# Key sums merged over two steps, scatters without a chain, and a replanned layer: one change to a two-layer recurrent-style kernel

## The chip, the cores and the metric

The kernel runs on one core of a Trainium2 chip. The metric is the device time of one execution in microseconds (us), the median of the runs shown. Profiles are of one execution each, with the time that it took.

## What is computed

Input `x` is [2, 2048, 256] in fp32, everything is fp32. Two layers, each `x = x + s * silu(f)`, on a layer norm of `x` without weights:

```
# layer 0
xn = layernorm(x)
s  = linear_attention(xn)                      # elu+1 features with rotary positions, 16 heads of 16, then @ W_out
h  = layernorm(xn)*ln1_g + ln1_b
y  = xn + softmax_attention(h) @ Wproj         # causal, rotary positions, 16 heads of 16, 2048 keys
h2 = layernorm(y)*ln2_g + ln2_b                # 4096 tokens
gates = softmax(h2 @ Wgate)                    # 8 experts, the best 2 of each token
pos = place of the token in its expert, in the order of the tokens   # room for 1024 a piece
moe = sum of both experts: gelu(h2 @ W1[e] + b1[e]) @ W2[e] + b2[e], times gate, none where pos >= 1024
x  = x + s * silu(y + moe)
# layer 1
xn = layernorm(x)
s  = softmax_attention(xn; q, k, v of 32 per head, 16 heads, causal) @ Wo
x  = x + s * silu(xn @ int4(kernel) + bias + xn @ a @ b)
```

## The kernel before, in words

There are three stages, in this order: layer 0 with both its attentions and the routing, the eight experts, layer 1.

**Attention in steps.** `run_attention` works for both layers. A group is one batch and four heads, eight groups in a layer. For a group and a chunk `c` of 256 queries, *pass A* (L534) forms scores of a tile of 128 queries against up to 512 keys, and DVE takes their maximum (L545, or L541 on the diagonal). `subtract` turns the maxima and folds them in: in layer 0 into `qt` (L782), in layer 1 by six small Pool instructions (L1433 to L1435), a turn (L1439), a copy (L1446) and a bf16 matmul on each score tile (L1453). *Pass B* (L560) forms the scores again with the keys on the partitions, two tiles of 128 keys (a pair `p`) at once, hides the future (L504), and ACT takes exp into `pt` (L572). Then `sum_keys` forms the sums over the keys: the weights of one `p` against `vt` (layer 0 L792, layer 1 L1466). In layer 0 `vt` carries a column of ones, so the sum of the weights comes with it. In layer 1 the heads fill all 32 columns; Pool adds the two key tiles (L1472, with a copy L1474 on the diagonal) into `ps`, and TensorE sums `ps` over the partitions (L1478, the total). DVE adds each result into `un` (L800; L1484). `finish` normalises, and in layer 0 calls `residual` (L841, L848) and, for every second chunk of the last group, `route`.

Scores use TensorE as four tiles of 32 rows, one head each. Sums use it as four tiles of 32 columns. All other work ("guests": projections, turns, linear attention, gates) uses the full array.

A step `u` of the loop has one pass A tile set and one pass B pair, four score tiles each, and the sums of an earlier step: two steps later in layer 0, three in layer 1 (`SUM_LAG`).

**The planner.** Every operation is a `Step` with an engine, an estimated cost, and what it reads and writes. `Plan.run` orders them by a beam search over a model of the engines, buffers and tiling modes, with handicaps by strand ("prep", "end", "moe", ...), and the program is then issued in that order by hand, with no other scheduler. Sums and scores are the main strand ("S") on TensorE. A guest may enter only in front of a main step that is marked open; before the change the first score of every step is open. The 8 PSUM banks `s` are shared by all. Parts of the linear attention are released by step number (`others`): batch 0 from step 4 on, batch 1 from step 150, one every 8 steps.

**Routing.** `route` takes four tiles of 128 tokens: statistics (L475, `roots` on Pool, L461), scaled tokens into `x2` (one slot), a turn and the gate matmul (L911), the choice of two experts and the places (small DVE instructions, a count on TensorE, L943), then eight indirect DMAs from Pool's queue (L972) that scatter rows to `slots_in` in DRAM. Each writes `slots_in`, and so waits for the one before to land. The experts load `xe` from `slots_in` (L1261), turn it (L1266), and multiply (L1272, L1278).

**Layer 1's start.** `mix` (L1332 to L1350) fetches each token's two expert rows with four indirect DMAs per two tiles, weighs and gates them; eight such parts for batch 0 come first, eight for batch 1 run beside the attention of batch 0, all partly on Pool.

Of the kernel before, what the change touches and what calls it, by code (L numbers as in the profile page):

```python
# [110 lines left out]
class Plan:  # L111
# [25 lines left out]
    BEAM, TRIALS, SPREAD = 4, 8, 0.4  # L137
# [180 lines left out]
def kernel(ctx: ExitStack, tc: tile.TileContext, i: dict, out: bass.AP):  # L318
# [60 lines left out]
    v8 = w0.tile([8, P], F32, name="v8")  # L379
    for n, name in enumerate(("ln1_g", "ln1_b", "ln2_g", "ln2_b")):  # L380
        nc.sync.dma_start(v8[2 * n : 2 * n + 2], i[f"L0_ffn_{name}"].rearrange("(k p) -> k p", p=P))
    b64 = w0.tile([E * 8, P], F32, name="b64")
# [17 lines left out]
    with tc.tile_pool(name="prelude", bufs=1) as pool:  # L400
        for n, c in enumerate((C_ID, C_AFTER)):
            m = bank().rearrange("p (q n) -> p q n", q=4)
            for q in range(4):
                rep = pool.tile([P, 4, 32], F32, name=f"rep{n}{q}")
                nc.vector.tensor_copy(
                    rep, ident[:, None, 32 * q : 32 * q + 32].to_broadcast([P, 4, 32])
                )
                nc.tensor.matmul(
                    m[:, q], rep.rearrange("p j d -> p (j d)"), cst[:, c : c + P], start=True, stop=True
                )  # L410
            if n == 0:
                nc.vector.tensor_copy(ident_h, m)
            else:
                nc.vector.tensor_copy(mask_h, m[:, :, None].to_broadcast([P, 4, 2, P]))
        tp = bank("t")
        nc.tensor.transpose(tp[:, :8], v8, ident[:8, :8])
        nc.vector.tensor_copy(cols, tp[:, :8])
        tp = bank("t")
        nc.tensor.transpose(tp[:, : E * 8], b64, ident[: E * 8, : E * 8])
        nc.vector.tensor_copy(b1c, tp[:, : E * 8])  # L420
# [33 lines left out]
    def norms(w, S):  # L454
# [4 lines left out]
        def root(dst, src, tmp):  # L459

            nc.gpsimd.tensor_tensor(dst, src, minus_half, ALU.pow)  # L461
            nc.gpsimd.tensor_tensor(tmp, dst, dst, ALU.mult)
            nc.gpsimd.tensor_tensor(tmp, tmp, src, ALU.mult)
            nc.gpsimd.tensor_scalar(tmp, tmp, -0.5, 1.5, ALU.mult, ALU.add)
            nc.gpsimd.tensor_tensor(dst, dst, tmp, ALU.mult)

        st, ag = w.tile([P, 4, 6], F32, name="ln_st"), w.tile([P, 4, 2], F32, name="ln_ag")
        va, tmp = w.tile([P, 4], F32, name="ln_v"), w.tile([P, 4], F32, name="ln_t")

        def stats4(strand, n0, name, r, m, r1=None):  # L470
            r, m = r[:, n0 : n0 + 4], m[:, n0 : n0 + 4]

            def moments():
                for n in range(4):
                    nc.vector.bn_stats(st[:, n], xr[:, n0 + n])  # L475
                for n in range(4):
                    nc.vector.bn_aggr(ag[:, n], st[:, n])

            def roots():
# [4 lines left out]
                if r1 is not None:  # L484
# [3 lines left out]
                    root(r1[:, n0 : n0 + 4], va, tmp)  # L488

            S(strand, "DVE", 2.2, moments, r=[("xr", n0 + n) for n in range(4)], w=["ln"])  # L490
            S(strand, "POOL", 2.4, roots, r=["ln"], w=["ln", (name, n0)])

        return stats4

    LAG = 1
    SUM_LAG = 3
# [16 lines left out]
    def run_attention(plan, make, prepare, subtract, sum_keys, finish, last_sum, before=None, others=()):  # L513
# [65 lines left out]
        sums, parts_left = {}, []  # L579
        for u in range(at + last_sum + 1):  # L580
# [29 lines left out]
            if first:  # L610
                first.open = True
            if a and t == 2 * c + 1 and k == t // 4:
                subtract(g, c, mx, parts)
            if b:
                for n, call in sum_keys(gb, cb, p, pt):
                    sums.setdefault(u + n, []).append(call)
                if p == cb:
                    sums[u + last_sum].append(lambda gb=gb, cb=cb: finish(gb, cb))
# [8 lines left out]
            while parts_left and u >= due:  # L627
                parts_left.pop(0)()
                due += every

# [4 lines left out]
    ps_first.close()  # L635
    with ExitStack() as sc:
# [13 lines left out]
        for vt in vts:  # L650
# [25 lines left out]
                x2=slots(wk, "x2", 1, [P, 4, D]), xl=slots(wk, "xl", 1, [P, 2, D]),  # L676
            ),
            dict(prep=-0.5, sub=-0.5, end=-0.2, moe=-0.1),
        )
        S = plan.step  # L680
        stats4 = norms(w, S)

        def normalise0(n0):
# [9 lines left out]
            stats4("prep", n0, "r", ln_r, ln_m, ln_r1)  # L693
# [90 lines left out]
        def sum_keys(G, c, p, pt):  # L784
            if p == 0:
                G.sums[c] = Buf("un")
            un, av = G.sums[c], Buf("s")

            def add():
                for n, (kj, q0, at) in enumerate(halves_of(c, p)):  # L790
# [828 lines left out]
```

## Time and profile before

| | us |
|---|---|
| median of 3 runs (lowest, highest) | 3627.52 (3627.36, 3629.56) |
| profiled execution | 3629.38 |
| its span, first to last instruction | 3627.6 |
| TensorE clock granted, mean | 0.961 of full |
| layer 0: last matmul of the key sums (L792) begins to end | 1439.8 to about 1441 |
| first expert matmul (L1272) | 1545.06 |

In lines of the page, `out<-in` are the program's names; "x" is a count; then follow the busy time in us, the mean of one in ns, and after the bar the idle time of the engine just before these instructions with what ended most of it. PE is TensorE's matmuls, PEld its weight loads, POOL is GpSimd. One fp32 matmul gives two matmul records. In a timeline or a chain, the first number is the start in us, the second the length.

### The profile page before, as it was taken

How to read it: one execution, taken by the hardware profiler on the slowest of the kernel's cores; microseconds unless marked ns; L12 is line 12 of the kernel's file. 1: busy time of each engine (PE TensorE's matmuls, PEld its weight loads, DVE VectorE, ACT ScalarE, POOL GpSimd, SP SyncE). 2: the span in 40 equal slices, each digit the busy share in tenths (PEclk: the TensorE clock that was granted, in tenths of full speed). 3: DMA queues.
4: the chain of work that ended last, by engine and by line, in shares of the span. 5: the costliest groups of instructions: out<-in, count | busy, mean ns of one | idle time of the engine just before them, and what ended most of it. 6: DMA issues, size and time to landing. Idle time of an engine off the chain costs nothing.

```text
span 3627.6 us, 83893 instructions
## 1 busy us (share of the span) xinstructions
PE 3423.8 (94%) x34834; PEld 2340.2 (65%) x34834; DVE 2311.2 (64%) x5937; ACT 1659.7 (46%) x3278; POOL 1395.6 (38%) x2134
## 2 busy tenths in 40 slices
PE   6999999999999999199999599999999999999999
PEld 4667777776677776166666356666666666666666
DVE  4777787878787877211111267777777657777776
ACT  2565555555555555011111155445445444444444
POOL 4453223333322212200000455666554345555555
PEclk7999999999999999599999789999999999999999
DMA  5000000000000000122220211110001010000000
GB/s 175 2 2 2 11 5 10 22 19 22 16 7 13 13 13 15 47 84 73 82 84 24 73 61 46 32 45 25 23 8 30 26 35 16 18 13 15 16 22 28
DMA packets 88031, 115.57 MB, mean 32 GB/s; under 512 B 9043, under 2 KB 67103, under 8 KB 87650
## 3 DMA queue, kind: packets, MB, share of 16 engines
q1 hardware_dynamic: 81506, 96.32, 8.1%
q0 software_dynamic: 6144, 13.88, 1.2%
q8 instruction: 274, 4.49, 0.5%
q14 instruction: 107, 0.88, 0.1%
HBM read 75.33 MB, written 37.75 MB: 31 GB/s over the span
## 4 chain that ended last, share of the span: by engine, by line
PE 87%; POOL 4%; DVE 4%; issue 3%; DMA 2%; ACT 1%; SPq 0%; POOLq 0%; ACTq 0%; DVEq 0%
PE s L560 16%; PE s L534 15%; PE s L1466 7%; PE s L792 7%; PE s L1272 6%; PE s L1278 6%; PE s L1478 3%; PE s L1395 3%; PE s L504 3%; PE s L729 3%; PE s L1453 2%; PE s L1520 2%; PE s L1410 2%; PE s L359 1%; PE s L1035 1%
## 5 line engine op out<-in xcount | busy, mean ns | idle before, releaser
L572 ACT ACTIVATE pt<-s 128x512 f32<-128x512 f32 (+1 forms) x2304 | 1160.5, 575 | 687.1 <-PE s L1453 281.1
L560 PE MATMUL s<-qt,kt 32*128 32x256 f32 (+1 forms) x9216 | 1266.1, 388 | 7.9 <-DVE un L798 3.2
L534 PE MATMUL s<-kt,qt 32*128 32x512 f32 (+3 forms) x5120 | 1236.4, 563 | 9.6 <-DVE mx L545 4.0
L545 DVE TENSOR_REDUCE mx<-s 128x1 f32<-128x512 f32 x1536 | 962.3, 682 | 195.9 <-PE s L534 101.8
L560 PEld LDWEIGHTS s<-qt,kt 32*128 32x128 f32 x9216 | 954.3, 186 | 58.4 <-ACT pt L572 10.4
L1472 POOL TENSOR_TENSOR ps<-pt 128x1024 f32<-128x1024 f32 (+1 forms) x288 | 608.5, 2115 | 502.2 <-PE s L1478 417.9
L534 PEld LDWEIGHTS s<-kt,qt 32*128 32x128 f32 x5120 | 484.0, 186 | 205.8 <-issue 94.9
L541 DVE CUSTOM_DVE_ANT_0 s<-s,cst 128x128 f32<-128x128 f32 (+3 forms) x1024 | 482.6, 513 | 106.2 <-PE s L534 84.6
L736 POOL TENSOR_TENSOR ra<-raw,rope 128x128 f32<-128x128 f32 x128 | 59.7, 466 | 667.7 <-ACT raw L748 602.1
L1466 PE MATMUL s<-pt,vt 128*32 128x256 f32 (+1 forms) x4608 | 297.9, 376 | 0.0
L792 PE MATMUL s<-pt,vt 128*32 128x256 f32 (+1 forms) x4608 | 296.4, 375 | 0.6 <-ACT pt L572 0.2
L1453 PE MATMUL s<-mh,ones_h 3*128 3x512 bf16 (+1 forms) x1152 | 287.6, 369 | 1.1 <-ACT mh L1446 1.1
L1281 DVE TENSOR_TENSOR ye<-s,b 128x256 f32<-128x256 f32 x64 | 27.2, 425 | 410.3 <-PE s L1278 410.3
L1332 POOL DMA_INDIRECT gx<-slots_out,back x64 | 62.7, 980 | 499.2 <-issue 496.8
L1273 ACT ACTIVATE hm<-s,b1c 128x512 f32<-128x512 f32 x128 | 87.9, 687 | 360.9 <-PE s L1272 360.9
L1272 PE MATMUL s<-xt,w 128*128 128x512 f32 x512 | 225.6, 599 | 7.1 <-DVE xt L1247 7.0
L1278 PE MATMUL s<-w,hm 128*128 128x256 f32 x1024 | 223.6, 379 | 0.0
L1466 PEld LDWEIGHTS s<-pt,vt 128*32 128x32 f32 x4608 | 121.3, 109 | 154.7 <-DVE mx L545 38.9
L1484 DVE TENSOR_TENSOR un<-un,s 128x512 f32<-128x512 f32 x224 | 153.4, 685 | 102.8 <-PE s L1478 101.9
L1278 PEld LDWEIGHTS s<-w,hm 128*128 128x128 f32 x1024 | 194.6, 190 | 33.3 <-issue 7.7
L792 PEld LDWEIGHTS s<-pt,vt 128*32 128x32 f32 x4608 | 121.0, 109 | 143.3 <-ACT pt L572 42.5
L504 PE MATMUL s<-mask_h,ident_h 32*128 32x256 bf16 x2048 | 192.9, 269 | 0.0
(256 smaller groups left out, 4160.2 us busy)
## 6 DMA issues: line engine op xcount, KB each, us to landing
w<-in_L_ffn_W_dram SPq DMA_DIRECT2D x16, 1024.0 KB, 5.4
gl<-g_dram SPq DMA_DIRECT2D x64, 256.0 KB, 2.6
slots_in<-zero SPq DMA_DIRECT2D x8, 1024.0 KB, 10.2
xe<-slots_in SPq DMA_DIRECT2D x16, 512.0 KB, 6.2
slots_out<-ye SPq DMA_DIRECT2D x16, 512.0 KB, 6.8
xr<-in_L_attn_x_dram SPq DMA_DIRECT2D x4, 1024.0 KB, 8.3
s_dram<-lo SPq DMA_DIRECT2D x16, 256.0 KB, 2.0
xl<-in_L_attn_x_dram SPq DMA_DIRECT2D x16, 256.0 KB, 2.7
```

Source lines behind the costliest of these rows:

```text
L504: nc.tensor.matmul(out, ident_h[r, q], mask_h[r, q].rearrange("p n k -> p (n k)"), start=False, stop=q == 3)
L534: nc.tensor.matmul(s.t[:, :w], g.qt.t[r, t * P : (t + 1) * P], g.kt.t[r, 512 * k : 512 * k + w], start=True, stop=True)
L541: nc.vector.tensor_tensor_reduce(s.t[:, :w], s.t[:, :w], causal[:, 512 - w :], 1.0, -3e38, ALU.add, ALU.max, to)
L545: nc.vector.tensor_reduce(to, s.t[:, :w], AX.X, ALU.max)
L560: nc.tensor.matmul(s.t[:, at], g.kt.t[r, kj * P : (kj + 1) * P], g.qt.t[r, QC * c + q0 : QC * (c + 1)], start=n == 0, stop=n == 1 and not ...
L572: S("B", "ACT", t_act(w), lambda: nc.scalar.activation(pt.t[:, j, :w], s.t[:, :w], AF.Exp, scale=0.25), r=[s], w=[(pt, j)])
L792: nc.tensor.matmul(av.t[32 * j : 32 * j + 32, q0:QC], vts[G.vn][:, kj, j], pt.t[:, j, at], start=n == 0, stop=n == 1)
L1272: nc.tensor.matmul(ps, w1[:, k, f * P : (f + 1) * P], xt[:, k], start=k == 0, stop=k == 1)
L1278: nc.tensor.matmul(ps[:, :D], hm[:, f, s * P : (s + 1) * P], w2[:, f], start=f == 0, stop=f == FF // P - 1)
L1453: return lambda: nc.tensor.matmul(s.t[:, :w_], ones_h[r], G.mh[c].t[r, 512 - w_ :], start=False, stop=last)
L1466: nc.tensor.matmul(av.t[32 * j : 32 * j + 32, q0:QC], G.vt.t[:, kj, j], pt.t[:, j, at], start=n == 0, stop=False,)
L1472: nc.gpsimd.tensor_tensor(ps.t[:, :, q0:], pt.t[:, :, same], pt.t[:, :, odd], ALU.add)
```

## The change

Six things, in the order of the diff below.

1. The key sums of two consecutive steps of a chunk (`pair`) go to TensorE as one set of matmuls into one bank, and DVE adds once per pair. In layer 1 Pool adds all four key tiles of the pair into one `ps`, so one total serves two steps. An odd last step is alone. The sums follow by one step in layer 0 (`SUM_LAG0`), by two in layer 1.
2. A step's first score is open to guests only where the step before had sums (or no pass B).
3. The scatters are declared independent of one another, wait only for the zeroed slots, and form a strand of their own ("send"); the first expert load waits for all of them. `x2` has two slots.
4. The last four token tiles are routed in two halves (`of` = 2).
5. The linear parts of batch 1 start at step 180, one every 7.5.
6. Layer 0 gets other handicaps, and the search draws its handicaps from a wider spread. The loads of the prelude go to a pool of their own; `xl` uses the slot of `hn`, `prod` that of `gates`.

```diff
-    BEAM, TRIALS, SPREAD = 4, 8, 0.4
+    BEAM, TRIALS, SPREAD = 4, 8, 0.6
...
     LAG = 1
-    SUM_LAG = 3
+    SUM_LAG0, SUM_LAG = 1, 2
...
-            if first:
+            if first and (u == 0 or closed):
                 first.open = True
+            closed = late or not b
...
             if b:
-                for n, call in sum_keys(gb, cb, p, pt):
+                pair = [*pair, (p, pt)] if p % 2 else [(p, pt)]
+                for n, call in sum_keys(gb, cb, pair, p % 2 == 1 or p == cb):
                     sums.setdefault(u + n, []).append(call)
...
-                x2=slots(wk, "x2", 1, [P, 4, D]), xl=slots(wk, "xl", 1, [P, 2, D]),
+                x2=slots(wk, "x2", 2, [P, 4, D]),
             ),
-            dict(prep=-0.5, sub=-0.5, end=-0.2, moe=-0.1),
+            dict(prep=-0.34, sub=-0.31, end=0.15, B=-0.18, V=0.13, A=-0.16, S=0.15, lin=0.1),
...
-                for n, (kj, q0, at) in enumerate(halves_of(c, p)):
+                for n, (pt, kj, q0, at) in enumerate(tiles):
                     for j in range(4):
                         nc.tensor.matmul(
-                            av.t[32 * j : 32 * j + 32, q0:QC], vts[G.vn][:, kj, j], pt.t[:, j, at], start=n == 0, stop=n == 1
+                            av.t[32 * j : 32 * j + 32, q0:QC], vts[G.vn][:, kj, j], pt.t[:, j, at],
+                            start=n == 0, stop=n == len(tiles) - 1,
                         )
...
-                if c % 2:
-                    route(G, c // 2)
+                if G.b == B - 1 and c >= NT // 2 - 2:
+
+                    route(G, 2 * c, 2)
+                elif c % 2:
+                    route(G, 2 * c - 2, 4)
...
                     def send(to=to, t=t):
-                        nc.gpsimd.indirect_dma_start(
+                        inst = nc.gpsimd.indirect_dma_start(
                             out=slots_in, out_offset=bass.IndirectOffsetOnAxis(ap=to[:, n0 + t : n0 + t + 1], axis=0),
                             in_=x2.t[:, t], in_offset=None, bounds_check=NSLOT - 1, oob_is_err=False,
-                        )
-
-                    S("moe", "POOL", 1.2, send, r=[("routes", n0), x2, "slots"], w=["slots"], lag=1.5)
+                        ).ins
+                        tc.declare_no_dep(inst, group="sends", reason="each token has rows of its own")
+                        tc.add_to_no_dep_group("sends", inst)
+                        sent.append(inst)
+
+                    S("send", "POOL", 1.1, send, r=[("routes", n0), x2, "zeros"], lag=2.0)
...
-            start, every = ((4, 7.5), (150, 8))[b]
+            start, every = ((4, 7.5), (180, 7.5))[b]
...
-                nc.sync.dma_start(xe, slots_in[r0 : r0 + 512, :].rearrange("(s p) d -> p s d", p=P))
+                load = nc.sync.dma_start(xe, slots_in[r0 : r0 + 512, :].rearrange("(s p) d -> p s d", p=P))
+                for inst in sent if e == h == 0 else ():
+                    tc.add_manual_dep(load.ins, inst.name, after, reason="every token is in its place")
...
+            def together():
+                if len(pair) == 1:
+                    nc.gpsimd.tensor_tensor(ps.t[:, :, q0:], pt.t[:, :, same], pt.t[:, :, odd], ALU.add)
+                    if q0:
+                        nc.gpsimd.tensor_copy(ps.t[:, :, :q0], pt.t[:, :, even.start : same.start])
+                else:
+                    nc.gpsimd.tensor_tensor(ps.t, ps.t, pt.t[:, :, even], ALU.add)
+                    nc.gpsimd.tensor_tensor(ps.t[:, :, q0:], ps.t[:, :, q0:], pt.t[:, :, odd], ALU.add)
+
+            calls = [(1, lambda: S("pair", "POOL", 2.2 * len(pair), together, r=[(pt, j) for j in range(4)], w=[ps]))]
+            if not last:
+                return calls
...
-                (1, lambda: S("pair", "POOL", 2.6, both, r=weights, w=[ps])),
                 (SUM_LAG, lambda: S(
-                    "S", "PE", t_row(2 * QC if p < c else P + QC), add,
-                    r=[(G.vt, 2 * p), (G.vt, 2 * p + 1), *weights], w=[(av, 0)], on="col",
+                    "S", "PE", t_row(columns), add,
+                    r=[*((G.vt, kj) for _, kj, _, _ in tiles), *((pt, j) for _, pt in pair for j in range(4))],
+                    w=[(av, 0)], on="col",
                 )),
```

## The prediction

> **What bounds the kernel now.** I read the busy shares, then the engines by stretch, then TensorE's timeline, then the waits at the seam between the layers. On the page:
>
> ```profile
> PE 3423.8 (94%) x34834; PEld 2340.2 (65%) x34834; DVE 2311.2 (64%) x5937; ACT 1659.7 (46%) x3278; POOL 1395.6 (38%) x2134
> ...
> L545 DVE TENSOR_REDUCE mx<-s 128x1 f32<-128x512 f32 x1536 | 962.3, 682 | 195.9 <-PE s L534 101.8
> ...
> L1472 POOL TENSOR_TENSOR ps<-pt 128x1024 f32<-128x1024 f32 (+1 forms) x288 | 608.5, 2115 | 502.2 <-PE s L1478 417.9
> ```
>
> TensorE sets the pace, but 94% overstates it: it contains waits between pipelined matmuls. The engines by stretch (after each stretch and its length: PE, PEld, DVE, ACT, POOL busy, then clock, DMA share, GB/s):
>
> ```profile
> 15.00:1444.00 1429.00, 1394.43 (x15137) 997.86 (x15138) 1097.05 (x3139) 797.04 (x1671) 462.78 (x1134) 0.98 0.06 19
> 1444.00:1545.00 101.00, 18.35 (x72) 14.61 (x70) 27.82 (x141) 8.69 (x18) 25.51 (x43) 0.53 0.17 57
> 1545.00:2012.00 467.00, 459.74 (x1657) 305.15 (x1656) 56.17 (x106) 89.14 (x129) 0.00 (x0) 1.00 0.20 65
> 2012.00:2100.00 88.00, 45.51 (x228) 26.77 (x231) 31.95 (x93) 22.88 (x37) 46.08 (x65) 0.67 0.27 88
> 2100.00:3627.00 1527.00, 1501.51 (x17729) 991.98 (x17725) 1090.60 (x2445) 741.66 (x1423) 859.01 (x880) 0.98 0.09 27
> ```
>
> So: attention of layer 0 (1429 us), a hole of 101 us in which TensorE works 18, the experts (467, untouched by the change), and layer 1 (1615). The hole is a Pool chain: the critical chain there runs through the scatters, each waiting for the one before to land.
>
> ```profile
> 1515.90 0.97 POOL slots_in L972
> 1516.87 1.22 issue
> 1518.32 2.22 DMA slots_in<-x,to
> 1521.29 0.97 POOL slots_in L972
> ...
> 1534.04 9.02 DMA xe<-slots_in
> ```
>
> Inside attention, TensorE alternates between 32-row tiles (scores), 32-column tiles (sums over keys) and the full array. I cut its records at each change of mode and took, for each run, the time to the start of the next run less the time in which its columns stream (0.83 ns per column and record, over four tiles in the tiled modes). A column run costs 0.15 us beyond its stream, a full-array run some 0.3, a row run of one step 0.33 to 0.37 when nothing waits, 0.6 in the mean. A row run of two steps back to back is dearer (layer 1; start, length):
>
> ```profile
> 3078.04 0.61 PE L1478 MATMUL s<-ps,ones 128*32 128x256 f32 x8
> 3078.58 0.69 PE L534 MATMUL s<-kt,qt 32*128 32x512 f32 x1
> ...
> 3084.38 1.07 PE L1466 MATMUL s<-pt,vt 128*32 128x256 f32 x16
> ```
>
> From 3078.58 to 3084.38 are 5.80 us for 3.84 us of stream: the second step needs banks that DVE (682 ns each, L545) has not emptied. Such runs cost 1.5 to 2.1 us beyond the stream.
>
> **What the Trainium skill says.** "TensorEngine Tiling (Array Packing)", Key Properties: changing the tiling mode drains the array; the 0.15 to 0.37 us agree. The same page, PSUM Bottleneck: four tiles at once speed up TensorE and not the emptying of PSUM; the run above agrees. "GPSIMD Engine Reference", 3.1: a two-input add is bound by its read port, 4497 ns for 2048 elements; here 1024 take 2357 ns (L1472), about half. "DMA: Bandwidth & Descriptors", Anatomy of one DMA: about 2.0 us fixed, mostly completion, so small DMAs should overlap; the scatters' 2.2 us agree.
>
> **The change part by part**, against the profiled execution (3629.4 us, span 3627.6; the median shown is 3627.5). Counts after are those of the compiled order of the changed program.
>
> *1. Fewer totals, layer 1.* One total per pair of steps: 288 fall to 160. A total streams 8 records of 256 columns in 0.43 us on TensorE, the bound: 128 x 0.43 = -55 us. Near certain in size.
>
> *2. Mode changes.* Column runs fall from 285 to 159 in layer 0 and from 287 to 161 in layer 1, row runs from 316 to 248 and from 313 to 239, full-array runs stay (241 to 240; 200 to 180). If each saved run gave back its clean cost: layer 0, 126 x 0.15 + 68 x 0.37 = -44; layer 1, 126 x 0.15 + 74 x 0.35 + 20 x 0.2 = -49. But row runs of two or more steps rise from 10 to 66 and from 19 to 74. With the mean excess of each kind in this trace (one step before a column run 0.60, before a full-array run 0.70, short ones 0.5 to 0.7, two steps 2.0 to 2.1, three 2.3 to 2.8) the sum is +13 in layer 0 (one step before a column run 182 to 32: -90; two steps 8 to 61: +104; the rest -1) and +7 in layer 1. The few two-step runs of layer 0 are mostly narrow ones; the one full one costs 1.47, which would make it -13. I take 0 and +7, ends -44 to +30 and -49 to +40.
>
> *3. Gathers.* 128 fewer DVE adds into `un` per layer: 128 x 0.414 = 53 us of DVE in layer 0, 128 x 0.685 = 88 in layer 1. DVE is busy 77% and 71% of these stretches and is what row runs wait for, so a part comes back: I take -10 in each, ends 0 and -30.
>
> *4. Pool's adds, layer 1.* Before: 224 x 2.357 + 64 x (1.271 + 0.627) = 650 us. After: 352 x 2.357 + 64 x 1.271 + 32 x 0.627 = 931, so +281. Over the layer that is 859 + 281 in some 1490 us, 77%, off the path. But not at the start: up to the 43rd of the 160 pairs Pool also fetches the experts' rows and finishes the mixing. Adding Pool's instructions in the new order (0.07 us between them, 1.25 per fetch as spaced in the timeline) gives 460 us, against 457 of TensorE by the costs above. Two engines equally full and coupled through the `pt` and `ps` slots cannot both be at 100%: I take +25, ends 0 and +60. Queued behind a pair's second add (4.7 us, was 2.4) are the pieces of the next maxima, which the scores of the next chunk need.
>
> *5. The hole.* From the last sum (1440.8) to the first expert matmul (1545.1) are 104 us, two whole routes one after the other, since one `x2` slot is free only after eight chained scatters (2.7 us each). After: scatters at 1 to 1.3 us apart, two `x2` slots, and a last route of two token tiles. From the rows of before: finish and residual 5.7; the first half-route's choice holds DVE and its first scatter stands ahead of the last roots on Pool, so these start near 12; roots 3.1, scale 1.0, turn, affine and gate 2.6, choice to `count` 5.5, places to the first scatter 2.7; the four scatters 5, landing 2.3, load issue 2.3, `xe` 9.0, turn 2: 47 us. So -57, ends -40 and -70. The linear parts that move later issue their loads and stores (SP) earlier than the last route, and the scatters no longer stall Pool in mid-layer (72 us of waits <-DMA at L972, covered by TensorE): 0. If that cover were gone, the last linear part would add its 6 us of TensorE work (L1086 and L1129, 1.9 each, three turns of 0.6).
>
> *6. Handicaps, wider search, prelude pool, slices of `minus_half`:* no instruction added; the order they give is what I counted. 0.
>
> Sum: -55 + 0 + 7 - 10 - 10 + 25 - 57 = -100. 3629 - 100 = 3529; against the median, 3528. What is late next: DVE's emptying of PSUM in layer 0, Pool in the first 420 us of layer 1.
>
> **Rivals.** *A, clean switches.* DVE, relieved, keeps up; row runs of two steps cost no more than others. For: the planner puts full-array work in the middle of many pairs (the row runs of one step before a full-array run rise from 36 to 70 in layer 0). Against: 5.8 us for 3.84 in full runs that repeat to 0.01 us. Then -44 - 49 - 55 - 57, Pool nil: 3424.
>
> *B, banks.* The two-step runs cost their full 2.1 us, DVE's relief gives nothing, Pool costs 45: +30 + 40 + 45 - 55 - 57: 3632 at the very worst, 3580 in the middle.
>
> *C, Pool's queue becomes layer 1's bound, slower than before.* Place: the six small Pool instructions per chunk (L1433 to L1435) from which the score matmuls of pass B get their maxima, now behind adds of 4.7 us. If each of 64 chunks waited one more add (2.36) in vain and the saturated start cost its 60: 151 + 60 - 25 more than my sum, 3714. It turns slower once the wait averages over 100 / 64 = 1.6 us a chunk. For: Pool as full as TensorE at the start. Against: before, `mh` is hardly waited for (L1453 idle 1.1 us), and later stretches leave Pool a fifth.
>
> *D, the merge does not take:* excluded by the compiled order (160 totals).
>
> **How the numbers follow.** Forecast 0.55 (3529, own range 3490 to 3565), A 0.17, B 0.16, C 0.10, and 0.02 that they cancel within 0.2%, about what a measurement of this kernel can tell from no change. The range reaches halfway to A and past the middle of B: 3450 to 3595. Faster takes all of the forecast, A and most of B: 0.86; same 0.03; slower 0.11.
>
> **What would show it.** 1: L1514 with 1280 records where L1478 had 2304. 2: two-step row runs at 1.5 to 2.1 us beyond their stream; if they are at 0.7, A. 4: in the first 420 us of layer 1, TensorE waiting for `ps` and Pool over 90% busy; if Pool stays under 80% there, the +25 is wrong. 5: about 47 us from the last sum to the first expert matmul. The prediction is wrong if the attention of layer 0 (1429 us) moves by over 45 us either way, or layer 1 (1615 us) by over 90.

## The result and the profile after

The changed kernel took 3565.68 us in the median of 4 runs (3563.22 to 3566.36), the kernel before 3628.54 (3627.36 to 3630.12) beside it on the same chip: 63 us less, ratio 0.9825 with a 95% interval of 0.9808 to 0.9842. The profiled execution took 3565.2 us with a span of 3563.4. The direction is that of the forecast, the size two thirds of it: 64.2 us of span, where the sum had 100. The time lies inside the whole range (3450 to 3595) and just past the end of the forecast's own (3490 to 3565).

To see where, I cut the span at four marks of each trace: the end of the last sum over keys of layer 0, the first and the last expert matmul, and the end of the span (us).

| stretch | before | after | change | forecast |
|---|---|---|---|---|
| layer 0, to its last sum | 1441.0 | 1453.0 | +12.0 | -10 |
| hole, to the first expert matmul | 104.0 | 56.4 | -47.6 | -57 |
| experts | 466.8 | 467.3 | +0.5 | 0 |
| layer 1 | 1615.8 | 1586.7 | -29.1 | -33 |
| span | 3627.6 | 3563.4 | -64.2 | -100 |

Layer 0 is the largest miss (22 us), the hole the second (9). Lines of the page of the kernel after, busy shares first, then groups (busy time, mean ns, idle before and its releaser):

```profile
PE 3381.1 (95%) x33814; PEld 2412.0 (68%) x33814; DVE 2193.3 (62%) x5726; ACT 1667.0 (47%) x3281; POOL 1679.8 (47%) x2238
...
L547 DVE TENSOR_REDUCE mx<-s 128x1 f32<-128x512 f32 x1536 | 958.6, 684 | 205.8 <-PE s L536 114.5
...
L1490 POOL TENSOR_TENSOR ps<-pt 128x1024 f32<-128x1024 f32 (+1 forms) x160 | 347.6, 2173 | 125.5 <-ACT pt L574 104.0
...
L1494 POOL TENSOR_TENSOR ps<-ps,pt 128x1024 f32<-128x1024 f32 x128 | 302.8, 2365 | 84.5 <-ACT pt L574 78.9
...
L1495 POOL TENSOR_TENSOR ps<-ps,pt 128x1024 f32<-128x1024 f32 (+1 forms) x128 | 268.1, 2095 | 10.0
```

TensorE has 1020 records fewer and is no less busy in share; Pool has 284 us more work (281 were worked out), VectorE 118 us less. The groups of TensorE alone show the totals and the subtraction of the maxima:

```profile
L1478 PE MATMUL s<-mh,ones_h 3*128 3x512 bf16 (+1 forms) x1152 | 316.9, 370 | 0.0
...
L1514 PE MATMUL s<-ps,ones 128*32 128x256 f32 x1280 | 99.9, 384 | 9.5 <-POOL ps L1495 7.8 <-POOL ps L1492 1.7
```

L1514 has the 1280 records that step 1 counted. It now waits for Pool (9.5 us, where L1478 of before waited 0.0). The maxima, which rival C had stuck in Pool's queue, hold up no score (the row with `mh`: 0.0), and the turn that brings them to TensorE waits for Pool less than it did. Its row before:

```profile
L1439 PE MATMUL s<-cst,mpad 128*128 128x128 f32 x128 | 27.4, 298 | 10.2 <-POOL mpad L1435 10.2
```

and after:

```profile
L1464 PE MATMUL s<-cst,mpad 128*128 128x128 f32 x128 | 26.5, 290 | 5.4 <-POOL mpad L1460 5.3
```

The engines by stretch, in the columns of the prediction's table. First its five stretches, with the marks of the new trace:

```profile
15.00:1453.00 1438.00, 1404.61 (x15146) 1051.44 (x15146) 1049.32 (x3052) 800.06 (x1677) 464.15 (x1145) 0.98 0.06 19
1453.00:1509.00 56.00, 16.12 (x70) 12.90 (x66) 27.94 (x146) 6.19 (x13) 21.24 (x39) 0.58 0.31 102
1509.00:1976.00 467.00, 459.92 (x1656) 305.05 (x1655) 56.41 (x105) 89.22 (x129) 0.00 (x0) 0.99 0.20 65
1976.00:2064.00 88.00, 46.19 (x220) 25.70 (x218) 30.65 (x93) 21.69 (x35) 45.91 (x64) 0.71 0.29 91
2064.00:3563.00 1499.00, 1450.11 (x16714) 1013.15 (x16712) 1021.33 (x2317) 749.54 (x1428) 1146.31 (x976) 0.97 0.09 27
```

Then four stretches of 100 us at the start of layer 1, where the forecast put Pool's price:

```profile
2200.00:2300.00 100.00, 91.90 (x944) 63.34 (x939) 65.01 (x153) 46.87 (x82) 76.63 (x75) 0.93 0.12 38
2300.00:2400.00 100.00, 92.71 (x1090) 64.15 (x1082) 76.57 (x152) 51.05 (x94) 89.99 (x79) 0.97 0.13 40
2400.00:2500.00 100.00, 88.75 (x883) 63.32 (x886) 73.81 (x168) 46.39 (x83) 79.76 (x81) 0.86 0.10 30
2500.00:2600.00 100.00, 100.00 (x1268) 72.48 (x1268) 69.53 (x153) 50.59 (x102) 80.34 (x64) 1.00 0.06 19
```

Pool (fifth busy number) is at 77 to 90% there and TensorE (first) at 89 to 93%; before, TensorE had 97.2, 97.1, 92.6 and 100.0 in the same stretches with Pool at 62 to 68. In the fourth stretch TensorE is full again. The prediction's sign for this price was Pool over 90% busy in the first 420 us of layer 1 and TensorE waiting for `ps`. Over those 420 us Pool is at 78% (327.4 us):

```profile
2064.00:2484.00 420.00, 388.59 (x3923) 264.81 (x3922) 298.74 (x638) 206.32 (x366) 327.38 (x312) 0.91 0.13 41
```

And of the waits of TensorE in them, 31 us in all (who waited for what, us, times, longest), those for `ps` are 2.0; most of the 9.5 of L1514 comes after 2560 us.

```profile
PE s L536 <- DVE mx L547: 9.5, 2, 5.7
...
PE s L1514 <- POOL ps L1492: 1.7, 2, 1.3
...
PE s L1514 <- POOL ps L1495: 0.3, 1, 0.3
```

The chain that ended last, in the hole:

```profile
1459.31 3.37 PE s L1151 x8
1462.68 0.81 PE s L930 x8
...
1467.85 0.60 DVE xr L866
...
1474.48 0.74 POOL ln_r L463
...
1491.02 0.38 POOL slots_in L991
...
1492.29 0.97 POOL slots_in L991
1493.25 0.30 issue
1493.56 2.27 DMA slots_in<-x,to
1496.10 0.39 SPq L1276
...
1497.66 0.62 SPq L1284
1498.33 9.07 DMA xe<-slots_in
```

The scatters stand 1.27 us apart and one landing (2.27) is left of the chain of landings. In front of it are the last linear part (L1151, 3.37 us at half clock) and two half routes; at the end the tokens of the first expert take 9.07 us.

Last, the row runs. In the method of the prediction (time from a run's start to the next run's, less its stream) layer 0 lost 331.2 us in its switches before and 344.2 after, layer 1 323.8 and 350.8. Runs of two steps: 61 in layer 0 with 1.91 us each, 63 in layer 1 with 1.67 us. Leaving out runs that a stretch of half clock touches, it is 1.75 and 1.41, against 0.60 and 0.58 for one step.

### The profile page after: what moved, and what is told of

Same layout as the page of the kernel before. It is cut to its first block, busy times and chain, and to the rows that moved or that the text cites. A ratio compares the mean times of both kernels' runs of the same rounds, so it can differ in the third digit from the quotient of the medians.

```text
span 3563.4 us, 81449 instructions
## 1 busy us (share of the span) xinstructions
PE 3381.1 (95%) x33814; PEld 2412.0 (68%) x33814; DVE 2193.3 (62%) x5726; ACT 1667.0 (47%) x3281; POOL 1679.8 (47%) x2238
## 4 chain that ended last, share of the span: by engine, by line
PE 84%; POOL 5%; DVE 5%; issue 3%; ACT 2%; DMA 1%; POOLq 0%; SPq 0%; DVEq 0%; ACTq 0%
PE s L562 16%; PE s L536 16%; PE s L804 7%; PE s L1297 6%; PE s L1303 6%; PE s L1508 6%; PE s L1420 3%; PE s L736 3%; PE s L506 3%; PE s L1478 2%; PE s L1514 2%; PE s L1556 2%; PE s L359 2%; PE s L1435 2%; PE s L1057 1%
## 5 line engine op out<-in xcount | busy, mean ns | idle before, releaser
L562 PE MATMUL s<-qt,kt 32*128 32x256 f32 (+1 forms) x9216 | 1329.0, 390 | 9.3 <-ACT pt L574 2.5
L536 PE MATMUL s<-kt,qt 32*128 32x512 f32 (+3 forms) x5120 | 1306.2, 563 | 21.1 <-DVE mx L547 11.4
L547 DVE TENSOR_REDUCE mx<-s 128x1 f32<-128x512 f32 x1536 | 958.6, 684 | 205.8 <-PE s L536 114.5
L562 PEld LDWEIGHTS s<-qt,kt 32*128 32x128 f32 x9216 | 1023.9, 186 | 66.9 <-ACT pt L574 13.2
L536 PEld LDWEIGHTS s<-kt,qt 32*128 32x128 f32 x5120 | 560.6, 187 | 170.0 <-issue 89.8
L1490 POOL TENSOR_TENSOR ps<-pt 128x1024 f32<-128x1024 f32 (+1 forms) x160 | 347.6, 2173 | 125.5 <-ACT pt L574 104.0
L1494 POOL TENSOR_TENSOR ps<-ps,pt 128x1024 f32<-128x1024 f32 x128 | 302.8, 2365 | 84.5 <-ACT pt L574 78.9
L1478 PE MATMUL s<-mh,ones_h 3*128 3x512 bf16 (+1 forms) x1152 | 316.9, 370 | 0.0
L804 PE MATMUL s<-pt,vt 128*32 128x256 f32 (+1 forms) x4608 | 272.6, 375 | 1.6 <-ACT pt L574 1.6
L1495 POOL TENSOR_TENSOR ps<-ps,pt 128x1024 f32<-128x1024 f32 (+1 forms) x128 | 268.1, 2095 | 10.0
L1508 PE MATMUL s<-pt,vt 128*32 128x256 f32 (+1 forms) x4608 | 271.7, 374 | 0.2 <-ACT pt L574 0.2
L1508 PEld LDWEIGHTS s<-pt,vt 128*32 128x32 f32 x4608 | 134.5, 110 | 138.9 <-issue 20.7
L804 PEld LDWEIGHTS s<-pt,vt 128*32 128x32 f32 x4608 | 134.5, 110 | 123.7 <-issue 25.0
```

The lines of the kernel that those rows point to most:

```text
L536: nc.tensor.matmul(s.t[:, :w], g.qt.t[r, t * P : (t + 1) * P], g.kt.t[r, 512 * k : 512 * k + w], start=True, stop=True)
L547: nc.vector.tensor_reduce(to, s.t[:, :w], AX.X, ALU.max)
L562: nc.tensor.matmul(s.t[:, at], g.kt.t[r, kj * P : (kj + 1) * P], g.qt.t[r, QC * c + q0 : QC * (c + 1)], start=n == 0, stop=n == 1 and not ...
L804: nc.tensor.matmul(av.t[32 * j : 32 * j + 32, q0:QC], vts[G.vn][:, kj, j], pt.t[:, j, at], start=n == 0, stop=n == len(tiles) - 1,)
L1478: return lambda: nc.tensor.matmul(s.t[:, :w_], ones_h[r], G.mh[c].t[r, 512 - w_ :], start=False, stop=last)
L1490: nc.gpsimd.tensor_tensor(ps.t[:, :, q0:], pt.t[:, :, same], pt.t[:, :, odd], ALU.add)
```

## The experiments

The kernels ran in four comparisons, each on another chip with the kernel before beside them: the next four experiments in the first, then the changed kernel again up to the halved work in the second, the three of "Layer 0 unmerged again" in the third, both edits in the fourth. A time without a range is that of a single run.

For the first comparison I had two theories of the miss in layer 0, with numbers in their expectations: two-step runs wait for VectorE, so that undoing the merge there gains (W); or the loss lies elsewhere in the layer, so that undoing it costs (L). After that comparison I set D beside them: a two-step row run fills sixteen score banks where each layer has eight (`s0` to `s7`), so its second step goes at the pace at which VectorE (maxima) and ScalarE (exponentials) empty them, and the merge in layer 0 saves nothing. Its rivals: ScalarE alone (S), the order over the row groups (O), and that layer 0 loses by its new plan and not by the merge. All spans are cut at the marks above; "excess" is the loss at switches.

The stretches of one and the same order of instructions differ too: the merged layer 1 took 1585.6 to 1594.0 us in seven profiles, and 1593.3 in the first comparison. So a difference in it of less than 8 us between comparisons says nothing.

### One step per set again in layer 0

```diff
         def sum_keys(G, c, pair, last):
-            if not last:
-                return []
+            pair = pair[-1:]
...
-    SUM_LAG0, SUM_LAG = 1, 2
+    SUM_LAG0, SUM_LAG = 2, 2
```

> The changed kernel with the key sums of layer 0 undone: one step per set of sums, two steps later, as before; layer 1, the scatters and the linear parts stay changed. By its compiled order, row runs of two or more steps in layer 0 fall from 66 to 21, column runs rise from 159 to 285. In the changed kernel the last key sum of layer 0 ends at 1453.0 us, in the kernel before at 1441.0. Theory W (two-step row runs wait until DVE has emptied banks, which eats the mode changes saved): the end comes at 1441 +- 8, the run at 3550 to 3562. Theory L (the 12 us come from the linear parts that moved late, the merge itself pays): the end stays at 1453 or goes up towards 1490, the run at 3565 to 3605.

3580.34 us (3579.47 to 3585.23), ratio 0.9881 (0.9865 to 0.9898); layer 0 1472.4, hole 50.6, layer 1 1593.3. This looked as if the merge in layer 0 were worth 15 us. It was not: see the repeats below.

### One step per set again in layer 1

```diff
         def sum_keys(G, c, pair, last):
+            pair, last = pair[-1:], True
...
-    SUM_LAG0, SUM_LAG = 1, 2
+    SUM_LAG0, SUM_LAG = 1, 3
```

> The changed kernel with the key sums of layer 1 undone (one step per set, 288 totals instead of 160, Pool adds two key tiles, sums three steps later); layer 0 stays changed. The gain of layer 1, 29 us, should go: layer 1 at 1616 +- 8 instead of 1586.7, the run at 3594 +- 8. If layer 1 gained by something else than the merge (the rule for where guests enter, the wider search), less than 15 us come back.

3615.73 us; layer 1 1619.0. Merging in layer 1 is worth 26 us net against the same layer in the experiment before, on the same chip (1593.3), and 32 against the first profile (1586.7): nearly all that the layer gained. But layer 0, untouched, ended at 1472.3 and not at 1453.0, which takes the total out of its interval (3594 +- 8).

### Pool without the fourth key tile

```diff
-                    nc.gpsimd.tensor_tensor(ps.t[:, :, q0:], ps.t[:, :, q0:], pt.t[:, :, odd], ALU.add)
+                    pass
```

> The changed kernel without Pool's last add of each two-step pair (the fourth key tile is left out of the weights' totals in layer 1), everything else in the same order. Pool loses 268 us of work in layer 1. Theory P (Pool, full at the start of layer 1, costs TensorE some 25 us or more): layer 1 falls by 20 to 45, nearly all of it before 2520 us; the run at 3520 to 3543. Theory W (banks alone): layer 1 falls by less than 6.

3557.94 us; layer 1 1566.3, 20.4 less than in the first profile and 27.0 less than in the first experiment, on the same chip. This kernel's totals lack a quarter of the keys of such a pair. The two stretches in which Pool was fullest:

```profile
2200.00:2300.00 100.00, 94.69 (x966) 63.74 (x960) 65.01 (x153) 49.20 (x86) 64.58 (x66) 0.95 0.12 38
2300.00:2400.00 100.00, 98.28 (x1143) 69.02 (x1136) 71.56 (x159) 52.54 (x99) 72.63 (x75) 0.95 0.13 40
```

Pool falls from 77 and 90% to 65 and 73, TensorE rises by 2.8 and 5.6 us. (Layer 1 starts 13 us later here; in stretches that are moved by as much, TensorE rises by 2.8 and 4.5.) The two-step excess is 1.75 us for 1.67 in all runs, 1.35 for 1.41 in those without half clock: Pool's price is hardly in them. It is 20 to 27 us, as step 4 had it (25). Set against each other instruction by instruction, 13 us of the 20 are gained by 500 us into the layer. TensorE's waits in the 420 us fall from 31 us to 14, those for VectorE's maxima from 9.5 to 0.8, those for `ps` from 2.0 to 0.4. So Pool's load came back for the most part through other waits than that for its sums; by which way is not shown.

### VectorE's maxima over half the keys, in layer 1

```diff
-                    nc.vector.tensor_reduce(to, s.t[:, :w], AX.X, ALU.max)
+                    nc.vector.tensor_reduce(to, s.t[:, : w // 2 if before else w], AX.X, ALU.max)
```

> The changed kernel with DVE's maxima over whole tiles in layer 1 taken over 256 of the 512 keys (the other half is left out of the maximum), in the same order. DVE's 768 reductions of 684 ns fall to about 410, 210 us less DVE work in layer 1. Theory W: the excess of two-step row runs in layer 1 falls from 1.67 us to below 1.0, that of one-step runs from 0.70 to below 0.5, layer 1 by 50 to 100 us. Theory P: less than 15 us, since Pool's load is the same.

3583.45 us; layer 1 1586.8, to 0.1 us the time of the first profile and 6.5 less than in the first experiment, on the same chip, though the maxima became cheaper there. VectorE's groups, by form; the 256-column row is layer 1's:

```profile
L547 DVE TENSOR_REDUCE mx<-s 128x1 f32<-128x512 f32 x768 | 479.7, 683 | 106.3 <-PE s L562 68.0 <-PE s L536 34.4 <-remote 1.4
L547 DVE TENSOR_REDUCE mx<-s 128x1 f32<-128x256 f32 x768 | 293.1, 419 | 180.7 <-PE s L536 144.8 <-PE s L562 28.0 <-PE s L1478 2.3
```

VectorE lost 186 us of work (958.6 - 479.7 - 293.1) and layer 1 0 to 6.5, where W had 50 to 100; the two-step excess stays at 1.68 (1.33 without half clock). W falls for layer 1.

Layer 0 was again late (1471.4), with the same instructions as after. Set against each other record by record, the two TensorE streams drift apart by 18 us, of which some 17 arise at three places, near 677, 890 and 1376 us. The engines by stretch around two of them, in the changed kernel:

```profile
660.00:680.00 20.00, 19.42 (x145) 13.12 (x141) 15.61 (x49) 6.20 (x14) 10.27 (x16) 0.83 0.15 53
680.00:700.00 20.00, 20.00 (x252) 15.22 (x248) 15.31 (x47) 13.53 (x28) 5.66 (x20) 1.00 0.01 2
...
900.00:920.00 20.00, 20.00 (x221) 13.59 (x220) 14.14 (x44) 9.49 (x22) 5.39 (x15) 1.00 0.05 15
```

and in the one with halved maxima:

```profile
660.00:680.00 20.00, 19.10 (x131) 12.50 (x129) 15.67 (x50) 6.13 (x13) 9.85 (x14) 0.79 0.15 53
680.00:700.00 20.00, 20.00 (x206) 14.41 (x205) 12.30 (x35) 12.31 (x26) 6.07 (x20) 0.87 0.00 1
...
900.00:920.00 20.00, 19.26 (x191) 13.90 (x194) 12.99 (x31) 10.81 (x22) 6.55 (x17) 0.83 0.01 2
```

The third number from the end is the granted clock. At 671 us both are put to half clock; in the one for 6.8 us, in the other for 13.7; near 900 us only the second is. Between 150 us and the end of layer 0 the changed kernel has 20.5 us of half clock, this one and the two with a layer unmerged 44.4, the one without the fourth tile 30.7. So totals of different comparisons could not be set against each other until the changed kernel had run again.

### The changed kernel again

> The changed kernel once more, with nothing altered, on the chip of this comparison. Three kernels with its layer 0 untouched (layer 1 unmerged, Pool's fourth tile left out, halved maxima) ended that layer at 1466 to 1472 us, where the changed kernel's own profile has 1453; at equal instructions they lost 13 to 19 us in three jumps (at 677, 780 to 890 and 1376 us), where the granted clock stood at half for longer. Chance theory (the half-clock stretches fall differently from chip to chip): layer 0 ends at 1464 to 1474 us and the median is 3573 to 3585. Build theory (it was the altered kernels' own doing): 1453 and 3561 to 3569.

3565.77 us (3564.72 to 3567.51), ratio 0.9828 (0.9812 to 0.9844); layer 0 1451.6, hole 56.4, layer 1 1590.5. In both comparisons it is the same. The late layer 0 was then the doing either of the first comparison (its chip or its hour) or of the altered kernels.

### Only the scatters, the half routes and the second x2

Both layers unmerged, planner settings, handicaps, steps open to other work and linear start as before (the scatters' new strand gets the handicap of "moe"); that is, the kernel before with these edits.

```diff
-                x2=slots(wk, "x2", 1, [P, 4, D]), xl=slots(wk, "xl", 1, [P, 2, D]),
+                x2=slots(wk, "x2", 2, [P, 4, D]),
...
+                if G.b == B - 1 and c >= NT // 2 - 2:
+                    route(G, 2 * c, 2)
...
+                        tc.add_to_no_dep_group("sends", inst)
```

> Both layers sum one step per column set as before, with the planner's settings of before; only the unchained scatters, the half routes and the second x2 buffer are kept. If these give the whole of the shorter hole: hole 50 to 60 us (before 104.0), layer 0 ends at 1441 +-6 and layer 1 takes 1616 +-6, in all 3572 to 3588, ratio to before 0.985 to 0.989. If the hole needs the replanned end of layer 0 (linear parts, merged sums): hole 65 to 85 us and 3595 to 3615.

3608.11 us (3607.49 to 3609.18), ratio 0.9946 (0.9929 to 0.9962); layer 0 1441.2, hole 85.1, layer 1 1613.2. The second theory holds, at the edge of its interval: these edits give 19 us of the hole's 48. The chain in its hole shows three routes after the last sum, of four tiles, two and two:

```profile
1450.36 1.05 POOL ln_r L463
...
1473.09 0.73 POOL ln_r L463
...
1491.30 0.74 POOL ln_r L463
...
1507.83 0.38 POOL slots_in L990
```

The first three rows are the roots of the three routes, the fourth is a scatter of the last one; in the changed kernel the route of four has its places before the last sum ends, and two halves follow. Which of them come before that sum is the plan's doing.

### ScalarE's exponentials halved, and VectorE's maxima as well

```diff
-                S("B", "ACT", t_act(w), lambda: nc.scalar.activation(pt.t[:, j, :w], s.t[:, :w], AF.Exp, scale=0.25), r=[s], w=[(pt, j)])
+                S("B", "ACT", t_act(w), lambda: nc.scalar.activation(pt.t[:, j, half(c, p)], s.t[:, half(c, p)], AF.Exp, scale=0.25), r=[s], w=[(pt, j)])
```

> ScalarE's exponentials cover only the even key tile in both layers (256 columns for 512); the odd tile's weights are replaced by the even's, so that half of the weights is left out of the result. TensorE's and VectorE's instructions keep their order. Theory D (in a two-step row run the second step's eight banks are those of the first, and TensorE waits for whichever of the two emptying engines is later, VectorE with four maxima of 0.62 us or ScalarE with four exponentials of 0.6 us per step, against 1.7 us of streaming): VectorE still stands in the way, two-step excess stays within 0.3 us of 1.78 in layer 0 and 1.38 in layer 1 (runs that the half clock doesn't touch). Theory S (ScalarE alone): it falls to 1.1 or less in both, and the layers are 25 to 60 us shorter together. Theory O (order of the matmuls over the four row groups, no bank): no change at all.

3520.29 us; layer 0 1445.2, layer 1 1555.4. Two-step excess 1.66 and 1.24 (untouched by half clock).

```diff
-                    nc.vector.tensor_reduce(to, s.t[:, :w], AX.X, ALU.max)
+                    nc.vector.tensor_reduce(to, s.t[:, : w // 2], AX.X, ALU.max)
```

> As the one with halved exponentials, and VectorE's row maxima of whole tiles read 256 of 512 columns in both layers as well (half of the scores is left out of the maxima, half of the weights out of the result). Theory D: two-step excess falls to 0.9 to 1.2 us in both layers, against twice the one-step 0.55 to 0.6; layer 0 is 30 to 50 us shorter, layer 1 15 to 40. Theory O: two-step excess stays at 1.78 and 1.38 within 0.2, and the layers lose under 15 us each.

3463.55 us; layer 0 1402.3 (49 less than the repeat on the same chip), layer 1 1536.8 (54 less). Two-step excess 1.17 and 1.03, twice the one-step 0.55 and 0.57, inside D's interval in both layers; that layer 1 gained 54 us, more than the 15 to 40 that D gave, is for the exponentials (below). So O and S fall, and D stands: once both engines are quicker, two steps back to back cost about what two single ones do. (In time the exponentials alone gained 41 us over both layers, inside S's 25 to 60; it is the excess that refutes S.) What is shown is that the pace of emptying sets the price; the number of banks was not varied. Nor is there a run with the halved work and layer 0 unmerged, so what the merge would then gain is not shown. TensorE's timeline of the changed kernel, from the start of a two-step run of layer 0 to the column run that follows it (start, length):

```profile
332.49 0.69 PE L536 MATMUL s<-kt,qt 32*128 32x512 f32 x1
...
336.51 0.81 PE L562 MATMUL s<-qt,kt 32*128 32x256 f32 x3
337.25 1.07 PE L804 MATMUL s<-pt,vt 128*32 128x256 f32 x16
```

VectorE's in the same microseconds:

```profile
332.63 0.43 DVE L811 COPY un<-s 128x256 f32<-128x256 f32 x1 [1.67 <-PE s L804]
332.97 0.68 DVE L1041 SCALAR_TENSOR_TENSOR lk<-la,lb 128x512 f32<-128x512 f32 x1
333.65 4.88 DVE L547 TENSOR_REDUCE mx<-s 128x1 f32<-128x512 f32 x8
```

and the same run of TensorE with both halved:

```profile
324.00 0.69 PE L542 MATMUL s<-kt,qt 32*128 32x512 f32 x1
...
327.91 1.06 PE L810 MATMUL s<-pt,vt 128*32 128x256 f32 x15
```

4.76 us for 3.41 of stream; VectorE works through it without a gap, eight maxima in 4.88 us. With exponentials alone halved the run still takes 4.76, with both 3.91. In layer 0 it is VectorE that is late: with the exponentials halved, halving its maxima gives 1445.2 - 1402.3 = 43 us, where the exponentials alone gave 6 (1451.6 - 1445.2). The maxima alone were not halved there. In layer 1 neither alone moves the two-step runs much; halving ScalarE's work gave 31 to 35 us, and VectorE's half, worth 0 to 6.5 by itself, 19 more. I had given the exponentials alone no such gain in layer 1; some 9 us of it lie in the two-step runs (63 with 0.14 us less each), the rest in runs of every kind and in 25 us less of half clock.

### Layer 0 unmerged again, tokens first, linear parts earlier

The first of these is the kernel of the first experiment, unaltered.

> The kernel with layer 0 unmerged (one step per column set there, all else as changed) once more. On the chip of its first run layer 0 ended at 1472 us, and so it did there in three kernels whose layer 0 was the changed one's; two chips agree on 1452 to 1453 for the unaltered changed kernel. Its layer 0 and hole together are the price of merging in layer 0 (1453.0 + 56.4 = 1509.4 with the merge). Theory D (a two-step run is held by the emptying of banks, so that the merge saves nothing): 1509 +-8 and a median of 3560 to 3575. As the record had it (merging costs nothing in row runs, -10 from fewer gathers): 1519 or more, 3572 or more. If the merge costs what its two-step row gave, +13: 1490 to 1500, 3548 to 3558.

3558.06 us (3554.85 to 3562.72), ratio 0.9805 (0.9789 to 0.9822), against 0.9881 (0.9865 to 0.9898) for the same kernel in the first comparison; layer 0 1455.4, hole 48.2, layer 1 1585.6. So this kernel's late layer 0 goes with the comparison and not with the code: there it has 44.4 us of half clock from 150 us on, here 23.9. Whether it is the chip or the hour is open. Layer 0 and hole together are 1503.6, between D's nothing (1509) and the price of +13 (1490 to 1500), and under the 1519 that the record's step implied; the median lies in W's interval of the first comparison (3550 to 3562), but the layer's end, 1455.4, does not (1441 +- 8): it is the hole that is shorter, so this doesn't speak for W. Merging in layer 0 costs some 4 to 6 us: it takes 2.4 to 4 us off the layer and its plan ends with a hole 8 us longer. As each of the two has an order of its own, that is the price of the merge with its plan.

```diff
...
+        first = fetch(0, 0)
         for e in range(E):
             w1 = wk.tile([P, 2, FF], F32, name="w1")
             nc.sync.dma_start(w1, w1_in[e])
...
-                xe = wk.tile([P, 4, D], F32, name="xe")
-                load = nc.sync.dma_start(xe, slots_in[r0 : r0 + 512, :].rearrange("(s p) d -> p s d", p=P))
...
+                xe = fetch(e, h) if e or h else first
```

> The first expert's tokens are loaded before its weights: SyncE's queue held the three weight loads in front of them (1496.10 to 1497.66 us), and then moved 512 KB of tokens beside 4 MB of weights in 9.07 us. If the tokens end the hole: 1.5 us earlier issue and 3 to 5 us faster landing, until the weights that now land later take over: hole 49 to 53 us (after 56.4), 3558 to 3564. If the weights are as late as the tokens, so that the one only takes the other's place: hole 55 to 58, 3563 to 3568.

3561.72 us (3556.67 to 3565.23), ratio 0.9815 (0.9797 to 0.9833), an interval that also holds the changed kernel's. The profile is plainer: layer 0 1453.2 and layer 1 1586.7 are the changed kernel's to 0.2 us, the hole is 49.4, that is 7.0 less. The chain's end:

```profile
1493.65 2.27 DMA slots_in<-x,to
1496.18 0.38 SPq L1277
...
1496.61 5.82 DMA w<-in_L_ffn_W_dram
...
1502.56 9.63 PE s L1303 x17
```

The tokens are no longer in it; the first expert's weights (5.82 us) are what comes last.

```diff
-            start, every = ((4, 7.5), (180, 7.5))[b]
+            start, every = ((4, 7.5), (150, 8))[b]
```

> The linear parts of the second batch start at step 150, one each 8 steps, as before the change, in place of 180 and 7.5, so that the last of them comes before the last sum over keys. The record had the last linear part's TensorE work as what the hole shows if its cover is gone: the chain of the changed kernel has it with 3.37 us at half clock (at 1459.31) between the turns and the gate of a half route. Cover theory: layer 0's end and the hole together 1503 to 1506 us (1509.4 with the late parts), 3558 to 3563. Nothing theory (the half route's other waits are next): 1509 +-3, 3563 to 3568. If the replanned layer is worse for it: over 1513.

3584.88 us (3583.21 to 3589.40), ratio 0.9876 (0.9859 to 0.9892); layer 0 1480.9, hole 45.6. The hole shrinks by 11 us, more than the cover theory said, and layer 0 grows by 28: the third theory. Moving one batch's parts by 30 steps gives a new order of the whole layer, with 366.0 us of excess for 344.2 and 49.2 us of half clock from 150 us on for 20.5, on a chip on which the other two kernels of this section have 20.5 and 23.9. So an order, too, can bring these stretches.

### Both edits

Layer 0 unmerged and the tokens first; both diffs are above.

> Layer 0 unmerged (one step per column set there) and the first expert's tokens loaded before its weights, layer 1 as changed. The two edits touch different stretches: unmerged, layer 0 and hole took 1503.6 us in the good run (1509.4 as changed), 1510 where the chip was less kind; tokens first shortened the hole by 7.0. If they add: layer 0 ends at 1455 +-5, hole 41 to 44, 3545 to 3556, ratio to before 0.976 to 0.980. If the unmerged layer's shorter hole and the tokens' earlier landing are the same microseconds: hole 47 to 50, 3555 to 3562.

3574.44 us (3567.78 to 3579.26), ratio 0.9875 (0.9858 to 0.9891), with the kernel before at 3622.46 beside it; layer 0 1468.6, hole 43.8, layer 1 1586.6. The hole is within what the first theory gave (41 to 44): there the two edits add, for the most part. The total is not, because layer 0 is 13 us late as in the first comparison, with 37.5 us of half clock. So I have no run in which this kernel beats both; that it would in another comparison is argued from its parts, not shown.

## Why the prediction was right in direction and a third too large

Step by step:

1. *Fewer totals, -55.* Right: the column stream of layer 1 fell from 355.0 to 300.4 us.
2. *Mode changes, 0 and +7.* Layer 1: its excess rose by 27.0 us, of which Pool's adds are 20 to 27; 0 to +7 is left. Layer 0: the excess rose by 13.0, which is the sum with the mean prices of before that the text worked out and did not take. But that is an accident: unmerged on the same plan, layer 0 has 348.4 us of excess. The plan put 17 on, and the merge, with the order that it brings, took 4 off. The prices were near: two-step runs 1.91 and 1.67 us for the 2.0 to 2.1 assumed.
3. *Fewer gathers, -10 and -10.* Layer 1: little. 186 us less of VectorE's work took 0 to 6.5 us off the layer, so that 88 us of gathers can hardly have given 10. Layer 0: not shown by itself. With the exponentials halved, 184 us less of VectorE's work there (1049.7 busy to 866.0) gave 43 us; at that rate 53 us of gathers would give 12, so the term may hold and be covered by the plan's cost.
4. *Pool's adds, +25.* Right in size, 20 to 27 measured, and for the most part in place. The way was wrong: Pool is at 78% and not over 90% in the first 420 us, just under the 80% at which, by the prediction's own sign, the +25 would be wrong, and TensorE waits 2.0 us for `ps` there. That the size came out is in part luck: taking Pool's work away shortens other waits of TensorE (31 us to 14).
5. *The hole, -57.* -47.6. The chain's pieces were priced well (landing 2.27 for 2.3, tokens 9.07 for 9.0). The term that failed is "these start near 12": the last half route's statistics begin 20.2 us after the last sum (1473.20) and its roots on Pool 21.2 us after it (1474.17), as the half route before it comes to its own roots only when the sums end and to its gate at 1462.68, behind the linear part (L1151) whose cover, as the text feared, is gone. That is the 9 us. With the linear parts earlier the hole is 11 us shorter. The cause was also in part misplaced: unchained scatters, half routes and `x2` alone give 19 us, the plan that brings a route forward the rest.
6. *Handicaps and wider search, 0.* This failed most. "No instruction added" was taken for no cost. With the scatters' edits and the settings of before, layer 0 ends at 1441.2; with the new plan, still unmerged, at 1455.4: +14, and the hole goes from 85.1 to 48.2. The plan buys 37 us of hole with 14 us of layer 0; both profiles have 23.9 us of half clock after the first 150, so it isn't that. "Plan" means here the handicaps and the search, the rule for open steps and the later linear parts, which step 5 had also put at 0. Which of them costs the 14 wasn't isolated.

The miss of 36 us is then 22 in layer 0 (14 of plan; the -10 that doesn't show is most of the rest), 9 in the hole and 4 in layer 1. Rival A (two steps cost no more than others) is refuted by the 1.75 us; its condition, emptying that keeps up, is what the halved work made. Rival C is refuted by the 0.0 us of L1478 and the 5.4 of L1464. B was near on the runs (1.91 and 1.67 us for its 2.1) and wrong on Pool (45).

What the Trainium skill says in "TensorEngine Tiling (Array Packing)", PSUM Bottleneck, that four tiles at once speed up TensorE and not the emptying of its banks, agrees with the halved work: 1.75 us to 1.17 in layer 0.

## What to carry to other kernels

Merging two steps into one column set saves what leaves the bound engine's stream (here 128 totals, 55 us); the mode changes that it saves are paid back if the merged row run needs more banks than there are, so look for whether the emptying engines work through such a run without a gap. A new order from a planner is an edit with a price of its own: run the old order with the other edits before giving it a zero. A full engine's price need not show as a wait for that engine: take its work away and see. And look at more than one comparison, or at equal instructions in the two traces, before a difference of half a per cent is given a cause.

## What the runs showed that I had not expected

- The half clock comes in stretches of about 3.4 us and multiples (3.4, 6.8, 10.2, 13.7), in the middle of layer 0 too. In the first and the last comparison the replanned layer 0 had 31 to 44 us of it after the first 150 us (17 to 27 in the others, the early linear parts aside) and ended 13 to 19 us later with the same instructions, while the kernel before ran beside it at 3624.42 and 3622.46 us, if anything faster. One kernel so had ratios of 0.9881 and 0.9805, with intervals that don't meet. In the twelve profiles whose layer 0 does its whole work there are 62 such stretches between 150 and 1440 us; 60 of them follow on 3.4 us in which TensorE was busy for 0.89 or less, as are only some 3% of the other pieces of 3.4 us. So the half clock follows pauses of TensorE, and a late layer can begin with a wait: of the 6 us lost near 890 us about half came before the clock fell. Why the same pauses bring more of it in one comparison than in another stays open.
- A load of 512 KB takes 9.07 us when its queue holds 2 MB of weights in front of it and 2 MB behind; issued first, it leaves the path.
- Scatters from Pool that don't wait for each other still stand 1.27 us apart: 0.97 busy, 0.30 to the next.
